# A graph network on one core: the rows of two relational tables as fp32r pairs instead of bf16 triples

## The chip, the cores and the metric

The kernel runs on one core of a Trainium2 chip. The metric is the device time of one execution in microseconds; the time before is the median of three runs.

## The reference, cut to what matters

Four graph layers follow one another on 3125 nodes of 128 features and 100,000 edges (sorted by destination). The change touches only the last of them, a relational network of two layers with eight kinds of edge:

```python
def rgcn_layer(x, src, dst, etype, W, W_root, b, num_rels):
    h = jnp.einsum('ni,rio->rno', x, W)
    msg = h[etype, src]
    seg = dst * num_rels + etype
    sums = jax.ops.segment_sum(msg, seg, num_segments=N * num_rels)
    cnt = jax.ops.segment_sum(jnp.ones(...), seg, num_segments=N * num_rels)
    mean = sums / jnp.maximum(cnt, 1.0)[:, None]
    return mean.reshape(N, num_rels, do).sum(axis=1) + x @ W_root + b
...
h = relu(rgcn_layer(x, src, dst, etype, W1, root1, b1, 8))   # 128 -> 256
y = rgcn_layer(h, src, dst, etype, W2, root2, b2, 8)         # 256 -> 128
x = _layernorm(x + y)
```

So for each node and each kind of edge the features of the source nodes are averaged, and the eight averages, each through its own weights, are added.

## The kernel before, in words

The 3125 nodes are 25 blocks of 128 (`NB`, `P`); a feature matrix lies in SBUF as 25 tiles of 128 nodes by 128 features. From 0 to about 430 us the kernel builds matrices of edge counts (bf16 `adj`, `adj_t`; uint8 `rel`, one for each relation) in HBM. Until about 850 us it runs the first three graph layers as products with `adj`. From there on it runs the two relational layers, and everything that is changed lies there.

**Two ways to sum over edges.** Destination blocks 0 to 14 (`ND = 15`, in chunks `DENSE` of 4, 4, 4 and 3 blocks) are done densely, blocks 15 to 24 by gathering.

*Dense*: `relation` (L873) takes one relation and one chunk. In each of five steps g it loads five source blocks of the uint8 counts (`load8`, SP's queue, L757, six buffers), casts them to fp32r (`cast8`, L767, on ScalarE or VectorE by a list, three buffers), and issues ten matmuls (L885): for each of the five source blocks two, with the hi and the lo fp32r part of the features as the stationary operand and 512 or 384 columns of counts moving. `split2` (L786) makes such a pair: hi is x rounded to fp32r on ScalarE (L789), lo the rest on VectorE (L790). A pair for all 25 blocks is a tile `hilo`, of which two buffers (tag `big`) exist; `hT` has the same tag. In layer 1 the features are x3 itself; in layer 2 each relation r has its own matrix, x3's successor hT times W2[r], which layer 1 has written to HBM.

*Gathered*: `gathered` (L893) is a generator. For each of the ten blocks it walks over 34 tiles of 128 edges (15 for the last block). For four tiles at a time VectorE builds a one-hot (L909) that says to which of 24 x 8 = 192 pairs of node and relation an edge belongs. GpSimd fetches the 128 source rows of a tile from a table in HBM (L919, an indirect DMA, 12 buffers `gx`). TensorE then adds gx times one-hot to an accumulator of 1024 columns in two PSUM banks (L927); where the 192 columns cross the border of the banks (column 512), the matmul is cut in two.

**The two tables.** `xt_d` holds x3, `ht_d` hT times W2 for eight relations. A row is kept as three bf16 parts that add up to the fp32 value, 768 bytes, so a gathered tile takes three bf16 matmuls. `store3` (L792) makes them: a = bf16(x) on ScalarE (L798), e = x - a on VectorE (L799), b = bf16(e) on ScalarE (L800), c = e - b on VectorE (L801), and one store on SP (L802). It is called for seven chunks of x3 (`stored`, L846) and, in `linear1` (L950), for 50 half-rows of four relations straight out of PSUM, after four matmul instructions each (L975; an fp32 product is two instructions in the trace).

**Reading the table densely.** In layer 2 `fetch` (L1018) brings one relation's 25 blocks back: five loads (`back`, two buffers, L1024), two additions on VectorE that rebuild fp32 (L1027, L1028), and `split2` into the pair.

**What sets the order.** `fill` (L866) advances the gathering generator at a rate, so that after each dense step of ten matmuls about two gathered tiles follow. `fetch(r + 1)` is called after the first chunk of relation r. The framework then orders each engine's queue at compile time by priority and its own estimates; in the trace `back` and `m8` loads alternate on SP's queue.

Of the kernel before, what the change touches and what calls it, by code (L numbers as in the profile page):

```python
# [21 lines left out]
P = 128  # L22
# [51 lines left out]
def listed(ctx: ExitStack, tc: tile.TileContext, p: dict, out: bass.AP, bad):  # L74
# [43 lines left out]

    inv_n = dram.tile([SB * 2 * P, R], F32, name="inv_n")

    xt_d = dram.tile([NP, 3 * D], BF, name="xt_d")
    ht_d = dram.tile([R * NP, 3 * D], BF, name="ht_d")

    xa = const.tile([P, NB, D], F32, name="xa")
    iota2 = const.tile([P, R * NB, 2], BF, name="iota2")
# [628 lines left out]
    with until_end:  # L754
# [34 lines left out]
            nc.scalar.copy(hi, x)  # L789
            nc.vector.tensor_sub(lo, x, hi.bitcast(F32))  # L790

        def store3(rows, x):  # L792

            n = x.shape[1]
            t = rp.tile([P, 4, 3, D], BF, name="t3", bufs=4)
            a, b, c = [t[:, :n, i, :] for i in range(3)]
            e = rp.tile([P, 4, D], F32, name="e3", bufs=3)[:, :n, :]
            nc.scalar.copy(a, x)  # L798
            nc.vector.tensor_sub(e, x, a)  # L799
            nc.scalar.copy(b, e)  # L800
            nc.vector.tensor_sub(c, e, b)  # L801
            nc.sync.dma_start(rows, t[:, :n].rearrange("p b i c -> p b (i c)"))  # L802


        def batchnorm(bst, i):
# [38 lines left out]
        hT = rp.tile([P, 2, NP], F32, name="hT", tag="big", bufs=2)  # L844

        def stored(m0, nb):  # L846
            store3(xt_d[m0 * P : (m0 + nb) * P].rearrange("(b p) c -> p b c", p=P), x3[:, m0 : m0 + nb, :])

        for c, (m0, nb) in enumerate(CH):
            t = bank(("acc", "x", "x", "x", "x", "mi", "mi")[c])  # L850
# [42 lines left out]
        def gathered(table, rows, put):  # L893
# [3 lines left out]
            for g in range(NG):  # L897
                b = ND + g
                wn = min(P, HL - b * P)
                iv = rp.tile([P, P * R], F32, name="invn", bufs=1)  # L900
                nc.scalar.dma_start(iv[:, : wn * R],
                                    bcast(inv_n.rearrange("n r -> (n r)")[b * P * R :], wn * R))
                acc = [bank("x") for _ in range(2)]
                seen = set()
                for t in range(GT[g]):
                    if t % 4 == 0:
                        nt = min(4, GM - t)
                        oh = rp.tile([P, 2, GW * R, 2], BF, name="oh", bufs=3)
                        ins = nc.vector.tensor_tensor(  # L909
                            oh[:, : nt // 2],  # L910
                            iota2[:, None, : GW * R, :].to_broadcast([P, nt // 2, GW * R, 2]),
                            gkey[:, g, t : t + nt].rearrange("p (j i) -> p j i", i=2)[:, :, None, :]
                            .to_broadcast([P, nt // 2, GW * R, 2]),
                            op=OP.is_equal,
                        )
                        if g == 0 and t < 12:
                            behind(ins, first_cast)
                    gx = rp.tile([P, 3, D], BF, name="gx", bufs=12)
                    nc.gpsimd.indirect_dma_start(  # L919
                        out=gx.rearrange("p i c -> p (i c)"), out_offset=None, in_=table[:],  # L920
                        in_offset=bass.IndirectOffsetOnAxis(ap=rows[:, g, t : t + 1], axis=0),
                    )
                    c0 = first(t) * R
                    ends = [c0] + ([512] if c0 < 512 < c0 + GW * R else []) + [c0 + GW * R]
                    for i in range(3):
                        for a, z in zip(ends, ends[1:]):
                            nc.tensor.matmul(  # L927
                                acc[a // 512][:, a % 512 : a % 512 + z - a], gx[:, i, :],
                                oh[:, t % 4 // 2, a - c0 : z - c0, t % 2],
                                start=(a // 512 not in seen), stop=(t == GT[g] - 1 and i == 2),  # L930
                                skip_group_check=True,
                            )
                            seen.add(a // 512)
                    yield
                parts = [(n, min(64, wn - n), acc[n // 64][:, : min(64, wn - n) * R],
                          iv[:, n * R : min(wn, n + 64) * R]) for n in range(0, wn, 64)]
                yield from put(b, wn, parts) or ()
                yield

        with tc.tile_pool(name="f_z", bufs=1, reuse_waits="tile") as zp:  # L940
# [9 lines left out]
            def linear1(z, m0, nb):  # L950
# [20 lines left out]
                for b in range(m0, m0 + nb):  # L971
                    for r in range(0, R, 4):
                        o = psum.tile([P, 512], F32, name="mi", tag="mi", bufs=2)
                        for a in range(2):
                            nc.tensor.matmul(o, hT[:, a, cols(b, 1)],  # L975
                                             wr[:, a, r : r + 4, :].rearrange("p r c -> p (r c)"),
                                             start=(a == 0), stop=(a == 1))
                        store3(ht_d.rearrange("(r n) c -> n r c", r=R)[b * P : (b + 1) * P, r : r + 4],
                               blocks(o))
                        yield  # L980

# [35 lines left out]
        with tc.tile_pool(name="f_hr", bufs=1, reuse_waits="tile") as hp:  # L1017
            def fetch(r):  # L1018

                pieces = pair()  # L1020
                for m0 in range(0, NB, 5):
                    t = hp.tile([P, 5, 3, D], BF, name="back", bufs=2)
                    r0 = r * NP + m0 * P
                    nc.sync.dma_start(t.rearrange("p b i c -> p b (i c)"),  # L1024
                                      ht_d[r0 : r0 + 5 * P].rearrange("(b p) c -> p b c", p=P))
                    f = hp.tile([P, 5, D], F32, name="f", bufs=2)
                    nc.vector.tensor_add(f, t[:, :, 0], t[:, :, 1])  # L1027
                    nc.vector.tensor_add(f, f, t[:, :, 2])  # L1028
                    split2(pieces, m0, 5, f)
                return pieces  # L1030

            oT = hp.tile([P, NP], F32, name="oT")
# [670 lines left out]
```

## Time and profile before

| | us |
|---|---|
| median of three runs | 2034.96 (2032.4 to 2036.95) |
| profiled execution, own time | 2027.4 |
| its span | 2025.5 |
| mean granted TensorE clock | 0.975 |
| L885 dense matmuls, 3200 | busy 792.3 |
| L927 gathered matmuls, 2208 | busy 227.1 |
| L767 casts, ScalarE 225 and VectorE 95 | busy 486.8 and 158.5 |
| L919 gathers, 321 in each layer | busy 366.1 and 326.2 |
| L909 one-hots, 170 | busy 90.3 |
| L1027 and L1028 rebuilding, 40 each | busy 32.6 and 32.4 |

The page gives busy time by engine and by line. Matmuls are pipelined, and the busy time of one counts its latency; what a matmul costs in a stream is the distance from one start to the next, which the chain of work in order of time shows. "PEld" is the load of the stationary operand, which can overlap a matmul. A line such as "PE acc L885 <- ACT m L767: 7.9, 14, 1.4" says that matmuls of L885 waited for casts of L767, 7.9 us in all, 14 times, at most 1.4 us.

### The profile page before, as it was taken

What the parts mean: (1) busy time and instruction counts of PE and PEld (TensorE: products, weight loads), DVE (VectorE), ACT (ScalarE), POOL (GpSimd) and SP (SyncE); (2) the same over time, 40 slices, a digit from 0 to 9 for tenths busy, and PEclk for the clock granted to TensorE, in tenths of its full rate; (3) what the DMA queues carried; (4) which work ended last, traced back from release to release, by engine and by line L of the source; (5) the groups of instructions that cost most, each with busy time, mean ns of one, the idle gap of its engine ahead of it and who ended that gap; (6) DMA issues with size and microseconds to landing.
All of it is one profiled execution on the core that took longest, in us unless ns stands there. A gap on an engine that the chain in (4) does not pass through costs nothing.

```text
span 2025.5 us, 30183 instructions
## 1 busy us (share of the span) xinstructions
PE 1794.3 (89%) x11523; PEld 1387.0 (68%) x11523; DVE 1205.1 (59%) x2055; ACT 1253.0 (62%) x1118; POOL 859.5 (42%) x717
## 2 busy tenths in 40 slices
PE   2677676669999999889999999999999999999897
PEld 1555555458888888667577567758757777777676
DVE  6999998777768863475455345435346444434424
ACT  3999997757888666663233333233338777777774
POOL 5315624120000000027777267706716666666664
PEclk9999998889999999999999999999999999999998
DMA  4766776667888887477677457737659887888773
GB/s 100 277 271 266 291 287 237 247 189 232 255 259 257 251 268 235 140 225 190 177 212 207 148 171 209 188 101 198 184 151 269 243 228 220 235 240 245 196 204 101
DMA packets 398932, 435.67 MB, mean 215 GB/s; under 512 B 27166, under 2 KB 355838, under 8 KB 398776
## 3 DMA queue, kind: packets, MB, share of 16 engines
q1 hardware_dynamic: 346274, 336.92, 53.0%
q0 software_dynamic: 33632, 67.07, 12.9%
q10 hardware_dynamic: 18870, 29.66, 4.9%
q8 instruction: 92, 1.51, 0.3%
q14 instruction: 64, 0.52, 0.1%
HBM read 319.07 MB, written 114.46 MB: 214 GB/s over the span
## 4 chain that ended last, share of the span: by engine, by line
PE 57%; ACT 4%; issue 3%; DVE 3%; another core or an unknown queue 2%; DMA 1%; ACTq 0%; SPq 0%; DVEq 0%
PE acc L885 30%; PE acc L628 8%; PE x L927 8%; PE mi L962 4%; PE mi L975 4%; ACT m L767 3%; PE mi L966 1%; DMA back<-ht_d 1%; PE mi L650 0%; PE x L836 0%; PE mi L740 0%; DVE hilo L790 0%; ACT mf L611 0%; DVE f L1027 0%
## 5 line engine op out<-in xcount | busy, mean ns | idle before, releaser
L885 PE MATMUL acc<-m,hilo 128*128 128x512 f32 (+1 forms) x3200 | 792.3, 393 | 22.8 <-ACT m L767 10.8
L767 ACT CAST m<-m 128x2560 fp32r<-128x2560 uint8 (+1 forms) x225 | 486.8, 2196 | 372.5 <-PE acc L885 148.7
L885 PEld LDWEIGHTS acc<-m,hilo 128*128 128x128 f32 x3200 | 576.5, 190 | 130.3 <-issue 17.6
L919 POOL DMA_INDIRECT gx<-xt_d,gsrc x321 | 366.1, 1140 | 638.5 <-DVE z L1007 413.7
L919 POOL DMA_INDIRECT gx<-ht_d,gsrc x321 | 326.2, 1016 | 200.1 <-issue 72.0
L628 PE MATMUL acc<-mf,halves 128*128 128x512 f32 (+1 forms) x1750 | 383.9, 377 | 11.5 <-DVE mf L613 11.0
L628 PEld LDWEIGHTS acc<-mf,halves 128*128 128x128 f32 x1750 | 320.4, 190 | 60.4 <-DVE mf L613 11.9
L611 ACT CAST mf<-m 128x2560 fp32r<-128x2560 bf16 (+1 forms) x126 | 263.7, 2100 | 67.3 <-PE acc L628 34.8
L927 PE MATMUL x<-oh,gx 128*128 128x192 bf16 (+5 forms) x2208 | 227.1, 239 | 5.5 <-issue 5.2
L927 PEld LDWEIGHTS <-gx 128*128 128x128 bf16 x2208 | 157.0, 97 | 99.2 <-issue 89.6
L767 DVE CAST m<-m 128x2560 fp32r<-128x2560 uint8 (+1 forms) x95 | 158.5, 1670 | 110.6 <-issue 40.3
L909 DVE TENSOR_TENSOR oh<-iota,gkey 128x768 bf16<-128x768 bf16 (+1 forms) x170 | 90.3, 532 | 208.5 <-PE x L927 143.2
L342 ACT CAST rb<-bld 128x800 uint16<-128x800 f32 x240 | 180.0, 847 | 6.5 <-PE bld L339 6.5
L339 PE MATMUL bld<-rhq,rlo 128*128 128x200 bf16 x960 | 124.2, 253 | 49.4 <-ACT rb L342 36.5
L290 POOL DMA_INDIRECT ew<-pk,ptr x26 | 72.7, 2797 | 193.9 <-DVE ptr L285 189.6
L339 PEld LDWEIGHTS <-rlo 128*128 128x128 bf16 x960 | 86.9, 98 | 85.3 <-issue 80.9
L613 DVE CAST mf<-m 128x2560 fp32r<-128x2560 bf16 (+1 forms) x49 | 97.5, 1989 | 70.1 <-PE acc L628 69.9
L191 DVE TENSOR_TENSOR lo<-iota,kT 128x4096 bf16<-128x4096 bf16 x50 | 114.2, 2283 | 11.1 <-PE bld L356 11.1
L191 DVE TENSOR_TENSOR rhq<-iota,kT 128x6400 bf16<-128x6400 bf16 x30 | 104.4, 3480 | 0.0
L975 PE MATMUL mi<-wr,hT 128*128 128x512 f32 x200 | 93.4, 601 | 2.5 <-issue 1.6
L359 ACT CAST at<-bld 128x800 bf16<-128x800 f32 x100 | 79.4, 835 | 20.7 <-PE bld L356 20.6
L270 POOL DMA_INDIRECT g<-in_dst,irow x26 | 76.6, 2947 | 22.9 <-DVE crow L265 9.8
(238 smaller groups left out, 1624.4 us busy)
## 6 DMA issues: line engine op xcount, KB each, us to landing
m<-rel SPq DMA_DIRECT2D x240, 320.0 KB
rel<-rb SPq DMA_DIRECT2D x120, 400.0 KB
m<-adj SPq DMA_DIRECT2D x60, 640.0 KB
m<-adj_t SPq DMA_DIRECT2D x40, 640.0 KB
m<-adj SPq DMA_DIRECT2D x45, 480.0 KB
adj_t<-at SPq DMA_DIRECT2D x25, 800.0 KB
adj<-av SPq DMA_DIRECT2D x25, 800.0 KB
ht_d<-t SPq DMA_DIRECT2D x50, 384.0 KB
```

The costliest lines, as they stand in the source:

```text
L191: return nc.vector.tensor_tensor(o, (iota2 if of is None else of)[:, None, :width, :].to_broadcast([P, PU // 2, width, 2]), k[:, :, None, ...
L339: nc.tensor.matmul(pt[:, k, : R * NB], lo2[:, j // 2, :, j % 2], hq[:, j // 2, :, j % 2], start=True, stop=True)
L342: nc.scalar.copy(rb[:, :, j0 : j0 + 4], pt[:, :, : R * NB].rearrange("p j q -> p q j"))
L611: nc.scalar.copy(v, src)
L613: nc.vector.tensor_copy(v, src)
L628: nc.tensor.matmul(acc[:, :w], x[:, 5 * g + k, :], mf[:, k, :w], start=(g == 0 and k == 0 and i == 0), stop=(more is None and g == 4 and k ...
L767: casts_by[on_act] = nc.scalar.copy(v, src) if on_act else nc.vector.tensor_copy(v, src)
L885: nc.tensor.matmul(acc[:, :w], x[:, 5 * g + k, :], m[:, k, :w], start=(g == 0 and k == 0 and i == 0), stop=(g == 4 and k == 4 and i == 1),)
L909: ins = nc.vector.tensor_tensor(oh[:, : nt // 2], iota2[:, None, : GW * R, :].to_broadcast([P, nt // 2, GW * R, 2]), gkey[:, g, t : t + nt ...
L919: nc.gpsimd.indirect_dma_start(out=gx.rearrange("p i c -> p (i c)"), out_offset=None, in_=table[:], in_offset=bass.IndirectOffsetOnAxis(ap ...
L927: nc.tensor.matmul(acc[a // 512][:, a % 512 : a % 512 + z - a], gx[:, i, :], oh[:, t % 4 // 2, a - c0 : z - c0, t % 2], start=(a // 512 no ...
L975: nc.tensor.matmul(o, hT[:, a, cols(b, 1)], wr[:, a, r : r + 4, :].rearrange("p r c -> p (r c)"), start=(a == 0), stop=(a == 1))
```

## The change

Both tables hold fp32 words, two parts of 128 to a row (1024 bytes), each an fp32r part. `store2` takes the place of `store3`: hi on ScalarE, lo on VectorE, one store. The table of x3 is stored from the two parts of `xs`, which exist already, with one DMA each. A gathered tile is two fp32r matmuls; the one-hots are built in fp32r, one tile after the other instead of in interleaved pairs; ten buffers `gx` instead of twelve. `fetch` loads the two parts of a relation straight into the pair, with ten DMAs, and has no arithmetic. Bitcasts to fp32 on both sides of the DMAs leave the bytes as they are.

```diff
@@ -118,8 +118,8 @@
 
     inv_n = dram.tile([SB * 2 * P, R], F32, name="inv_n")
 
-    xt_d = dram.tile([NP, 3 * D], BF, name="xt_d")
-    ht_d = dram.tile([R * NP, 3 * D], BF, name="ht_d")
+    xt_d = dram.tile([NP, 2 * D], F32, name="xt_d")
+    ht_d = dram.tile([R * NP, 2 * D], F32, name="ht_d")
 
     xa = const.tile([P, NB, D], F32, name="xa")
     iota2 = const.tile([P, R * NB, 2], BF, name="iota2")
@@ -789,17 +789,14 @@
             nc.scalar.copy(hi, x)
             nc.vector.tensor_sub(lo, x, hi.bitcast(F32))
 
-        def store3(rows, x):
+        def store2(rows, x):
 
             n = x.shape[1]
-            t = rp.tile([P, 4, 3, D], BF, name="t3", bufs=4)
-            a, b, c = [t[:, :n, i, :] for i in range(3)]
-            e = rp.tile([P, 4, D], F32, name="e3", bufs=3)[:, :n, :]
-            nc.scalar.copy(a, x)
-            nc.vector.tensor_sub(e, x, a)
-            nc.scalar.copy(b, e)
-            nc.vector.tensor_sub(c, e, b)
-            nc.sync.dma_start(rows, t[:, :n].rearrange("p b i c -> p b (i c)"))
+            t = rp.tile([P, 4, 2, D], F32R, name="t2", bufs=3)
+            hi, lo = [t[:, :n, i, :] for i in range(2)]
+            nc.scalar.copy(hi, x)
+            nc.vector.tensor_sub(lo, x, hi.bitcast(F32))
+            nc.sync.dma_start(rows, t[:, :n].rearrange("p b i c -> p b (i c)").bitcast(F32))
 
 
         def batchnorm(bst, i):
@@ -844,7 +841,9 @@
         hT = rp.tile([P, 2, NP], F32, name="hT", tag="big", bufs=2)
 
         def stored(m0, nb):
-            store3(xt_d[m0 * P : (m0 + nb) * P].rearrange("(b p) c -> p b c", p=P), x3[:, m0 : m0 + nb, :])
+            rows = xt_d[m0 * P : (m0 + nb) * P].rearrange("(b p) (i c) -> i p b c", p=P, i=2)
+            for i, x in enumerate(xs):
+                nc.sync.dma_start(rows[i], x[:, m0 : m0 + nb, :].bitcast(F32))
 
         for c, (m0, nb) in enumerate(CH):
             t = bank(("acc", "x", "x", "x", "x", "mi", "mi")[c])
@@ -905,29 +904,28 @@
                 for t in range(GT[g]):
                     if t % 4 == 0:
                         nt = min(4, GM - t)
-                        oh = rp.tile([P, 2, GW * R, 2], BF, name="oh", bufs=3)
+                        oh = rp.tile([P, 4, GW * R], F32R, name="oh", bufs=3)
                         ins = nc.vector.tensor_tensor(
-                            oh[:, : nt // 2],
-                            iota2[:, None, : GW * R, :].to_broadcast([P, nt // 2, GW * R, 2]),
-                            gkey[:, g, t : t + nt].rearrange("p (j i) -> p j i", i=2)[:, :, None, :]
-                            .to_broadcast([P, nt // 2, GW * R, 2]),
+                            oh[:, :nt],
+                            iota2[:, None, : GW * R, 0].to_broadcast([P, nt, GW * R]),
+                            gkey[:, g, t : t + nt, None].to_broadcast([P, nt, GW * R]),
                             op=OP.is_equal,
                         )
                         if g == 0 and t < 12:
                             behind(ins, first_cast)
-                    gx = rp.tile([P, 3, D], BF, name="gx", bufs=12)
+                    gx = rp.tile([P, 2, D], F32R, name="gx", bufs=10)
                     nc.gpsimd.indirect_dma_start(
-                        out=gx.rearrange("p i c -> p (i c)"), out_offset=None, in_=table[:],
+                        out=gx.rearrange("p i c -> p (i c)").bitcast(F32), out_offset=None, in_=table[:],
                         in_offset=bass.IndirectOffsetOnAxis(ap=rows[:, g, t : t + 1], axis=0),
                     )
                     c0 = first(t) * R
                     ends = [c0] + ([512] if c0 < 512 < c0 + GW * R else []) + [c0 + GW * R]
-                    for i in range(3):
+                    for i in range(2):
                         for a, z in zip(ends, ends[1:]):
                             nc.tensor.matmul(
                                 acc[a // 512][:, a % 512 : a % 512 + z - a], gx[:, i, :],
-                                oh[:, t % 4 // 2, a - c0 : z - c0, t % 2],
-                                start=(a // 512 not in seen), stop=(t == GT[g] - 1 and i == 2),
+                                oh[:, t % 4, a - c0 : z - c0],
+                                start=(a // 512 not in seen), stop=(t == GT[g] - 1 and i == 1),
                                 skip_group_check=True,
                             )
                             seen.add(a // 512)
@@ -975,7 +973,7 @@
                             nc.tensor.matmul(o, hT[:, a, cols(b, 1)],
                                              wr[:, a, r : r + 4, :].rearrange("p r c -> p (r c)"),
                                              start=(a == 0), stop=(a == 1))
-                        store3(ht_d.rearrange("(r n) c -> n r c", r=R)[b * P : (b + 1) * P, r : r + 4],
+                        store2(ht_d.rearrange("(r n) c -> n r c", r=R)[b * P : (b + 1) * P, r : r + 4],
                                blocks(o))
                         yield
 
@@ -1018,15 +1016,10 @@
             def fetch(r):
 
                 pieces = pair()
+                rows = ht_d[r * NP : (r + 1) * NP].rearrange("(b p) (i c) -> i p b c", p=P, i=2)
                 for m0 in range(0, NB, 5):
-                    t = hp.tile([P, 5, 3, D], BF, name="back", bufs=2)
-                    r0 = r * NP + m0 * P
-                    nc.sync.dma_start(t.rearrange("p b i c -> p b (i c)"),
-                                      ht_d[r0 : r0 + 5 * P].rearrange("(b p) c -> p b c", p=P))
-                    f = hp.tile([P, 5, D], F32, name="f", bufs=2)
-                    nc.vector.tensor_add(f, t[:, :, 0], t[:, :, 1])
-                    nc.vector.tensor_add(f, f, t[:, :, 2])
-                    split2(pieces, m0, 5, f)
+                    for i, x in enumerate(pieces):
+                        nc.sync.dma_start(x[:, m0 : m0 + 5, :].bitcast(F32), rows[i][:, m0 : m0 + 5])
                 return pieces
 
             oT = hp.tile([P, NP], F32, name="oT")
```

## The prediction

> **What bounds the kernel now.** I read the page first: busy shares, then the chain that ended last.
>
> ```profile
> PE 1794.3 (89%) x11523; PEld 1387.0 (68%) x11523; DVE 1205.1 (59%) x2055; ACT 1253.0 (62%) x1118; POOL 859.5 (42%) x717
> PE 57%; ACT 4%; issue 3%; DVE 3%; another core or an unknown queue 2%; DMA 1%; ACTq 0%; SPq 0%; DVEq 0%
> ```
>
> TensorE holds the chain. The change begins at about 854 us (x3) and ends with the program, so I then read the chain in order of time inside the two relational layers (861 to 1521 and 1521 to 2025 us).
>
> ```profile
> 1100.66 2.36 PE acc L885 x10
> 1103.02 0.53 PE x L927 x6
> 1103.55 2.36 PE acc L885 x10
> ...
> 1179.15 0.56 PE x L927 x12
> ...
> 1503.27 2.00 PE mi L962 x16
> ...
> 1505.49 1.79 PE mi L962 x16
> ...
> 1507.50 1.78 PE mi L975 x4
> ```
>
> These give the spacing of matmuls, which is what PE pays. A dense fp32r product of 512 columns: 236 ns. Six gathered bf16 matmuls (two tiles) of 192 columns: 88 ns each. Twelve of a tile pair cut at column 512 of the accumulator: 47 ns each. An fp32 pass (the trace has two for each fp32 product) of 64 columns: 112 ns. One of 512 columns: 429 to 445 ns. Tiles and dense steps alternate without a gap, so a nanosecond of gathered matmul is a nanosecond of layer 1.
>
> Last, what PE waits for in layer 2, and the DMA load there (columns: window, PE, PEld, DVE, ACT, POOL busy, clock, DMA share, GB/s).
>
> ```profile
> PE mi L1042 <- DVE oT L1061: 8.3, 2, 5.8
> PE acc L885 <- ACT m L767: 7.9, 14, 1.4
> PE acc L885 <- issue: 6.4, 15, 1.0
> PE x L927 <- issue: 4.7, 9, 0.9
> ...
> PE acc L885 <- DVE hilo L790: 1.1, 1, 1.1
> ```
> ```profile
> 1550.00:1600.00 50.00, 48.01 (x293) 38.64 (x293) 24.28 (x38) 41.13 (x24) 35.60 (x34) 1.00 0.88 254
> 1750.00:1800.00 50.00, 47.92 (x288) 37.96 (x287) 24.46 (x43) 39.11 (x23) 33.81 (x34) 1.00 0.89 253
> ```
>
> PE idles about 33 us in all of layer 2, and the DMA engines are nearly full. So PE is the bound, with DMA close behind in layer 2 alone.
>
> **What the Trainium skill says.** "TensorE: Matmul & The Clock Gate", LDWEIGHTS: a load takes its columns over 1.2 GHz, so 107 ns for 128; the section on weight-path modes adds that the fast load is for types other than FP32. The trace agrees: fp32 loads last 190 ns, bf16 ones 97, and the 112 ns of a 64-column fp32 pass is far above its 53 ns of columns (as 429 ns for 512 scales), so the load sets it. "VectorE: DVE Perf Modes", what auto-detection checks: two results a cycle for two-source operations only where every tensor is 16-bit. The trace agrees: 768 bf16 elements take 553 ns (L909), 640 with an fp32 output 824 (L1027). "DMA: Bandwidth & Descriptors", issuing engines are not separate queues: all queues share the same 16 engines. The trace agrees, in that one DMA share covers SP's, ACT's and POOL's.
>
> **The change, part by part.** Durations are of the profiled execution: 2027.4 us, a span of 2025.5 and 1.9 around it. The median is 2034.96, 7.6 more, which I add at the end.
>
> *Gathered matmuls (L927).* Two parts instead of three. There are 2208 now = 642 tiles x 3 + 94 tiles cut in two x 3. Now: 548 whole tiles x 3 x 88 = 145 us, 94 cut ones x 6 x 47 = 26, together 171. After: 548 x 2 + 94 x 4 = 1472. No fp32r matmul in the trace is narrower than 384 columns (178 ns, 10 in 1.78 us on the chain), so I bound it. From below: the columns at the 384-column rate, 89 ns, less than the load, so 112 ns: 1472 x 0.112 = 165 us, 6 less than now. From above: as an fp32 product, two passes of 0.84 ns a column, 322 ns for 192: 548 x 2 x 322 = 353, the cut ones 65 with the load as floor, together 418 us, **247 more**. I take 112: fp32r ran in one pass at 384 and 512 with nearly the same ns a column (0.46), so nothing shown makes a narrower one run twice. **-6 us**.
>
> *One-hots (L909).* Output in fp32, so one result a cycle at 1.08 ns an element (from 512 in 686 to 640 in 824): 768 in 962 ns, +409 on 152, about +200 on 18: +66 us of DVE in both layers, and nothing at the other end (unchanged 553). DVE is busy 20 to 29 of 50 us there, and three buffers of four tiles run ahead of PE: 0 on the path. If that cover went, each tile would pay 0.1 us, 66 us in all; since a pair of tiles comes every 2.9 us on PE, I count nothing.
>
> *x3 stage.* store3's two ACT and two DVE steps for seven chunks go (t, e, t: 0.5 to 0.69 us each): 8 us of ACT and 9 of DVE. From 861 to 876 us DVE is solidly busy and PE's L885 has gaps of 2.2, 0.9, 0.3, 0.2 and 1.4 us, 5 in all; then it runs 119 products without one. The cast ends that last gap, so not all goes: **-4 us**. SP issues 14 stores in place of 7, 0.36 us each: 2.5 us ahead of m8 loads whose next casts have six buffers.
>
> *store2 (50 blocks of linear1).* L800 (0.62) and L801 (0.69) go. PSUM is still freed after one ACT and one DVE read, L798 0.58 and L799 0.69. Now ACT's L800 waits for L799 ahead of the next L798: 0.58 + 0.69 + 0.62 = 1.9 us a block against 1.72 on PE (4 x 429). Afterwards 1.3. The waits PE shows for it are 3.7 us (DVE e 2.1, issue 1.6); the last store before layer 2 also leaves 1.3 sooner. **-4 us**. Stores of 512 KB for 384: 25600 packets at 46 ns for 36 in the trace, 16 us of the 16 engines in layer 1, where their share is 0.44 to 0.79: hidden.
>
> *Fetch.* L1027, L1028, L790 (40 x 0.82 each, 97 us of DVE) and L789 (28 us of ACT) go. What PE waits for in layer 2 is only partly theirs: hilo 1.1, casts behind hilo copies some of 7.9 and 6.4. I credit 5 us. Against it: 80 DMAs of 320 KB for 40 of 480. Each now writes the hilo pair itself, so **SP waits** for the last L885 of the relation two before, where ACT and DVE did; behind it on SP's queue stand the m8 loads (L757), for them ACT's casts, for those PE. Packets in the trace: 768 B take 36 ns, 512 B 27. 25600 x 36 becomes 51200 x 27: over 16 engines 58 to 86 us, +29. I take -5 from the freed engines and +5 from this: 0.
>
> *Gathers (L919).* 1024 B a row for 768. POOL's issue is by row (0.95 us, a pitch of 1.25), so unchanged. One engine's share is now packets of 1536 and 4608 B, 65 + 221 = 286 ns; a third more, 381: +31 us of DMA in each layer. Ten gx buffers for twelve still reach seven steps of 2 tiles less two: about 14 us ahead, where a gather needs a few. 0 on the path.
>
> Sum: -6 - 4 - 4 + 0 = -14, so 2013 for the profiled execution and **2020** for the median.
>
> **Rivals.**
> 1. *Narrow fp32r matmuls run at the fp32 rate* (slower). +247 us on PE; about 20 of it fills idle time of layer 2, and 8 of savings stay: 2027.4 + 247 - 20 - 8 = 2246, median about **2250**. For it: no fp32r product under 384 columns is shown. Against it: the constant ns a column above. It decides as soon as a 192-column product costs over about 130 ns (1472 x 0.018 = 26 us above my price, more than the other savings). A halfway price (165 ns) would give some 2095.
> 2. *DMA becomes the bound of layer 2.* Now 0.777 of 514 us = 399 us there; + 29 + 31 = 459, 0.89. In the stretch with fetches, at 0.80 to 0.89 now, it is 0.96. One fetch is 6400 packets x 27 / 16 = 10.8 us of all engines, 15 beside the gathers, as one burst ahead of the m8 loads, whose six buffers hold 6 x 2.9 = 17 us less what SP waits for PE. If that wait is a step or two, PE stalls up to 6 us in each of seven relations, +42: 2020 + 42 - 5 = about **2057**. For it: the shares. Against it: the order on SP is interleaved already (back and m8 loads alternate in the queue's timeline), and a chunk's first pieces are needed first.
> 3. *Nothing much moves*: the gathered matmuls cost 124 ns, savings off the path: **2035**.
>
> **How the numbers follow.** Forecast 0.48, rival 1 (all prices well over 130 ns) 0.27, rival 2 0.19, rival 3 0.06. The forecast's own range is 2004 to 2031. For 8 in 10 the range must take in rival 2 and half of rival 1: 2004 to 2250, which leaves out 0.14 above and some 0.04 below. 0.2% is 4 us, about what a measurement tells from no change. Faster 0.45 (0.03 of the forecast falls within 0.2%), same 0.09, slower 0.46.
>
> **What would show it.** Right: six gathered matmuls (0.53 us) become four in 0.45 between dense steps of 2.36; L909 about 960 ns; no gaps at 861 to 876; layer 1 shorter by 10 us or more; layer 2 within 10 us of its 504 with a DMA share near 0.9. Wrong: four gathered in 0.6 us or more (rival 1), or "PE acc L885 <- ACT m L767" of tens of us in layer 2, with casts waiting for m<-rel behind hilo<-ht_d (rival 2).

## The result and the profile after

| | before | after |
|---|---|---|
| median of 20 runs each, same chip | 2032.0 us (2024.1 to 2037.69) | 2037.74 us (2027.13 to 2043.84) |
| ratio after to before | | 1.0029 (95% 1.0016 to 1.0042) |
| span of the profiled execution | 2025.5 | 2037.6 |
| mean granted TensorE clock | 0.975 | 0.964 |

The kernel is slightly slower, by 0.3%. I had forecast 12 to 15 us less. Lines of the changed kernel carry other numbers: dense products L884, gathered ones L925, casts L767, the ten loads of a fetch L1022, linear1's products L960 and L973.

The page first: busy shares and the chain.

```profile
PE 1786.8 (88%) x10787; PEld 1439.2 (71%) x10787; DVE 1143.3 (56%) x1871; ACT 1195.0 (59%) x1014; POOL 853.8 (42%) x717
PE 54%; issue 3%; ACT 3%; DMA 2%; another core or an unknown queue 2%; DVE 2%; SPq 1%; ACTq 0%; POOLq 0%; DVEq 0%
```

PE's part of the chain falls from 57 to 54%, though the span grows: PE has less to do and waits more. The chain in order of time, in the dense part of layer 1:

```profile
1095.63 2.35 PE acc L884 x10
1097.98 0.42 PE x L925 x4
1098.40 2.34 PE acc L884 x10
...
1103.69 0.42 PE x L925 x4
```

Four gathered matmuls in 0.42 us, 105 ns each, where six took 0.53. The same view at the end of layer 1, where the kernel before had sixteen 64-column passes in 1.79 us:

```profile
1492.64 3.45 DMA gx<-xt_d,gsrc
...
1496.86 4.44 DMA gx<-xt_d,gsrc
...
1503.97 3.31 PE mi L960 x16
```

PE waits for gathers, and afterwards a pass costs 207 ns instead of 112. Last, layer 2: PE's waits (us in all, times, longest), and three stretches (same columns as before, the last three are clock, DMA share, GB/s).

```profile
PE acc L884 <- ACT m L767: 18.4, 12, 6.1
PE acc L884 <- issue: 8.8, 7, 3.9
PE x L925 <- issue: 6.7, 8, 3.5
```
```profile
1550.00:1600.00 50.00, 46.54 (x242) 40.47 (x241) 15.01 (x21) 34.24 (x17) 32.42 (x34) 0.93 0.88 242
1650.00:1700.00 50.00, 43.62 (x219) 37.41 (x218) 11.47 (x15) 32.54 (x16) 31.35 (x31) 0.90 0.91 256
1750.00:1800.00 50.00, 46.29 (x239) 39.66 (x240) 15.58 (x31) 34.51 (x18) 33.99 (x34) 0.97 1.00 290
```

The waits for casts are not many, 12 instead of 14, but long: up to 6.1 us for 1.4. And the clock, which was 1.00, is 0.90 to 0.97.

**Where the time went.** I cut both traces at the starts of matmuls: the first and last dense product of layer 1, the product for oT (hT times the root weights, with which layer 2 begins; its own 10.3 to 10.6 us stand in no row), and the dense products of layer 2 by relation. "Half clock" is the time for which the trace's clock record shows TensorE at half speed; for layer 2 it takes in a last piece of 9 to 13 us, which reaches 2 us past the program's end. The pair on the right (runs e13 and e14 below) was taken on another chip, side by side.

| us | before | after | e13, before | e14, after |
|---|---|---|---|---|
| dense part of layer 1 | 590.3 | 580.3 | 587.8 | 578.6 |
| end of layer 1 (last dense product to product for oT) | 59.4 | 74.5 | 62.1 | 72.8 |
| relation 0, after that product | 55.6 | 51.7 | 55.2 | 51.7 |
| relations 1 to 7 | 434.9 | 443.1 | 425.4 | 442.8 |
| from there to the end | 13.6 | 16.4 | 13.2 | 16.6 |
| half clock: end of layer 1 | 0 | 20.5 | 3.4 | 20.5 |
| half clock: layer 2 | 26.5 | 51.2 | 12.1 | 50.2 |

So the predicted 10 us of the dense part came, and were given back at the end of layer 1 and in layer 2.

### The profile page after: what moved, and what is told of

The parts are those of the page before. It is cut to its first block, busy times and chain, and to the rows that moved or that the text cites. A ratio compares the mean times of both kernels' runs of the same rounds, so it can differ in the third digit from the quotient of the medians.

```text
span 2037.6 us, 28569 instructions
## 1 busy us (share of the span) xinstructions
PE 1786.8 (88%) x10787; PEld 1439.2 (71%) x10787; DVE 1143.3 (56%) x1871; ACT 1195.0 (59%) x1014; POOL 853.8 (42%) x717
## 4 chain that ended last, share of the span: by engine, by line
PE 54%; issue 3%; ACT 3%; DMA 2%; another core or an unknown queue 2%; DVE 2%; SPq 1%; ACTq 0%; POOLq 0%; DVEq 0%
PE acc L884 29%; PE acc L628 7%; PE x L925 7%; PE mi L960 4%; PE mi L973 4%; ACT m L767 2%; SPq L1022 1%; DMA m<-rel 1%; PE mi L964 1%; PE mi L1029 1%; DMA hilo<-ht_d 0%; DMA gx<-xt_d,gsrc 0%; PE mi L650 0%; DMA inv<-inv_d 0%
## 5 line engine op out<-in xcount | busy, mean ns | idle before, releaser
L884 PE MATMUL acc<-m,hilo 128*128 128x512 f32 (+1 forms) x3200 | 778.9, 390 | 34.9 <-ACT m L767 19.7
L767 ACT CAST m<-m 128x2560 fp32r<-128x2560 uint8 (+1 forms) x225 | 486.2, 2196 | 414.9 <-PE acc L884 130.0
L884 PEld LDWEIGHTS acc<-m,hilo 128*128 128x128 f32 x3200 | 581.5, 192 | 136.7 <-ACT m L767 22.2
L917 POOL DMA_INDIRECT gx<-xt_d,gsrc x321 | 370.4, 1154 | 646.9 <-PE acc L884 408.5
L908 DVE TENSOR_TENSOR oh<-iota,gkey 128x768 fp32r<-128x768 bf16 (+1 forms) x170 | 154.9, 913 | 275.1 <-PE x L925 171.6
L925 PEld LDWEIGHTS x<-oh,gx 128*128 128x128 f32 x1472 | 216.8, 193 | 52.2 <-issue 23.8
L925 PE MATMUL x<-oh,gx 128*128 128x192 f32 (+5 forms) x1472 | 228.2, 280 | 13.3 <-issue 6.7
L767 DVE CAST m<-m 128x2560 fp32r<-128x2560 uint8 (+1 forms) x95 | 159.1, 1676 | 88.8 <-issue 28.9
L191 DVE TENSOR_TENSOR lo<-iota,kT 128x4096 bf16<-128x4096 bf16 x50 | 114.1, 2282 | 13.0 <-PE bld L356 11.6
L973 PE MATMUL mi<-wr,hT 128*128 128x512 f32 x200 | 94.7, 615 | 5.9 <-issue 5.9
L798 DVE TENSOR_TENSOR t<-mi,t 128x512 fp32r<-128x512 f32 x50 | 34.5, 691 | 110.4 <-ACT t L797 87.9
```

Of the source, the lines that this page charges most:

```text
L191: return nc.vector.tensor_tensor(o, (iota2 if of is None else of)[:, None, :width, :].to_broadcast([P, PU // 2, width, 2]), k[:, :, None, ...
L767: casts_by[on_act] = nc.scalar.copy(v, src) if on_act else nc.vector.tensor_copy(v, src)
L884: nc.tensor.matmul(acc[:, :w], x[:, 5 * g + k, :], m[:, k, :w], start=(g == 0 and k == 0 and i == 0), stop=(g == 4 and k == 4 and i == 1),)
L908: ins = nc.vector.tensor_tensor(oh[:, :nt], iota2[:, None, : GW * R, 0].to_broadcast([P, nt, GW * R]), gkey[:, g, t : t + nt, None].to_bro ...
L917: nc.gpsimd.indirect_dma_start(out=gx.rearrange("p i c -> p (i c)").bitcast(F32), out_offset=None, in_=table[:], in_offset=bass.IndirectOf ...
L925: nc.tensor.matmul(acc[a // 512][:, a % 512 : a % 512 + z - a], gx[:, i, :], oh[:, t % 4, a - c0 : z - c0], start=(a // 512 not in seen), ...
```

## The experiments

**Theory A.** (i) At the end of layer 1, 13 gathered tiles of the last block stand behind the last but one linear1 in PE's order; ten buffers hold ten of them, and PE waits for the rest. (ii) In layer 2 a fetch is now ten loads in one go; SP is held up by them, the counts behind them come late, then the casts, then PE. Later I added (A2) that a long wait of PE is followed by half clock. **Rivals**: the DMA engines' bytes bound layer 2; the order set at compile time and the clock make the end of layer 1 longer, not the buffers; the inv loads on ScalarE's queue, behind which casts stand, are what is late in layer 2.

The chain in order of time of the changed kernel shows one such fetch, and SP's queue its issues:

```profile
1652.99 2.00 SPq L1022
...
1655.04 2.49 SPq L1022
...
1657.58 8.24 DMA hilo<-ht_d
...
1665.90 0.33 ACTq L779
...
1669.95 2.33 ACT m L767
...
1672.33 4.64 PE acc L884 x10
```
```profile
1636.48 9.35 SPq L757 DMA_DIRECT2D m<-rel  x3
1645.88 16.51 SPq L1022 DMA_DIRECT2D hilo<-ht_d  x10
1662.50 17.74 SPq L757 DMA_DIRECT2D m<-rel  x10
```

A load of counts takes SP 0.36 us to issue, a load of the fetch 1.4 at the median and up to 4.0; ten hold SP for 16.5 us. The first load of counts after them leaves at 1662.5, and the cast that needs it starts at 1669.95, 7.4 later. 24 us without counts against six buffers of 2.8 us each leaves PE some 7 us short; it waits 6.1, and its next ten products take 4.64 us instead of 2.35. In the kernel before the same queue alternates:

```profile
1588.77 1.17 SPq L1024 DMA_DIRECT2D back<-ht_d  x2
1590.59 3.85 SPq L757 DMA_DIRECT2D m<-rel  x2
1596.07 0.36 SPq L1024 DMA_DIRECT2D back<-ht_d  x1
1596.53 0.49 SPq L757 DMA_DIRECT2D m<-rel  x1
```

Times below are ratios to the kernel before on the same chip, with 95% intervals. The runs fell on five chips, on which the kernel before took 2021.5 (e1 to e4), 2030.8 (e5 to e8), 1968.5 (e9 to e12), 2019.4 (e13 to e16) and 2031.2 us (e17, e18). The unaltered changed kernel was run beside e5 to e8 and e13 to e16 alone; elsewhere its 1.0029 to 1.0057 are from other chips. Stage times are from one profiled execution each, and that can lie off the median: by 5 us in e2 and e3, and by 11 in e4, whose profile is the slowest of its 13 runs.

**e1: twelve buffers.**
```diff
-gx = rp.tile([P, 2, D], F32R, name="gx", bufs=10)
+gx = rp.tile([P, 2, D], F32R, name="gx", bufs=12)
```
To make room, root2 is loaded later and `m` has a smaller pad.


> The changed kernel with twelve gx buffers instead of ten; to make room, root2 is loaded in the second layer's pool and the pad of m is 4 instead of 8. Theory A (the end of layer 1 pays for the two missing buffers: 13 tiles of the last block are left after the last but one linear1, ten are there, three are fetched while PE waits): the stretch from the last dense product of layer 1 to the product for oT falls from 85 to about 77 us, and the median by 6 to 8, to about 2031. Theory B (the end of layer 1 is longer because of the slower TensorE clock and the order set at compile time): at most 2 us, about 2036. Theory C (everything that was lost lies in layer 2): within 1 us of 2037.


Measured: 1.0036 (1.0022 to 1.0051). The stretch of 85 us, which counts the oT product itself, became 81. PE takes 8.4 us for the last gathered tiles instead of 10.5, of which waits for gathers are 3.7 instead of 4.8 (the expectation of e6 calls the whole 10.5 and 8.4 a wait). The time shows no gain. Half of what theory A said in the trace, nothing in the ratio.

**e2: ten buffers in the kernel before.**
```diff
-gx = rp.tile([P, 3, D], BF, name="gx", bufs=12)
+gx = rp.tile([P, 3, D], BF, name="gx", bufs=10)
```


> The kernel before with ten gx buffers instead of twelve, nothing else. Theory A: its last block has twelve tiles left at that place, ten are there, two must be fetched while PE waits, so the 70 us of the end of layer 1 become 75 to 77 and the median 2032 becomes about 2038. Theories B and C: within 1.5 us of 2032.


Measured: 1.0020 (1.0011 to 1.0030), about 4 us; the 70 us became 79. The timeline of PE:

```profile
1503.41 0.43 PE L927 MATMUL x<-oh,gx 128*128 128x128 bf16 x6 [1.88 <-DMA gx<-xt_d,gsrc]
1503.68 0.30 PE L956 MATMUL mi<-ident,xa 128*128 128x128 f32 x1
1504.93 3.50 PE L962 MATMUL mi<-zg,w 128*128 128x64 f32 x16 [0.94 <-DVE zg L991]
```

The missing two buffers cost 1.9 us of waiting, and then the 64-column passes take 3.50 us instead of 2.00: the clock is half for 10 us. This, alone in the kernel before, is the loss at the end of layer 1 in small. The 79 is from a profile 5 us above the median, so the ratio is the safer size.

**e3: the fetch spread.** One load after each dense step of chunks 1 and 2.
```diff
-for m0 in range(0, NB, 5):
-    for i, x in enumerate(pieces):
-        nc.sync.dma_start(...)
+def parts():
+    for m0 in range(0, NB, 5):
+        for i, x in enumerate(pieces):
+            nc.sync.dma_start(...)
+            yield
...
 fill(work, rate)
+next(each, None)
```


> The changed kernel with the ten loads of a fetch issued one after each dense step of chunks 1 and 2 instead of all after chunk 0; same bytes, same packets, same number of DMAs. Theory A (the burst holds SP's queue and the semaphores of earlier DMAs, so the uint8 counts and the inv loads come late): the long chunks 1 of relations 2, 5, 6 and 7 (20 to 25 us) go back to 14 to 17, relations 1 to 7 take 435 instead of 443 us, median about 2030. Rival (the DMA engines are the bound of layer 2 by their bytes): no change, 2036 to 2039. If SP's order makes the next relation's first piece late, slower: 2045.


Measured: 1.0003 (0.9989 to 1.0018), relations 1 to 7 in 436.9 us. Near what theory A said: with the same bytes some 5 us less than the changed kernel's 1.0029, which is from another chip. But not every long chunk 1 went: that of relation 6 took 23.8 us, that of relation 7 19.0.

**e4: hi and lo side by side.** Five loads with 1024-byte packets.
```diff
-t = rp.tile([P, 2, NB, D], F32R, name="hilo", tag="big", bufs=2)
+t = rp.tile([P, NB, 2, D], F32R, name="hilo", tag="big", bufs=2)
```


> The changed kernel with hi and lo of a block side by side in SBUF, so that a fetch is five DMAs with 1024-byte packets instead of ten with 512, still all at once; the store of x3 is one DMA for a chunk instead of two. Packet time of the fetches falls from 2 x 27 to 46 ns a row, 15 per cent of 86 us, 13 us of all engines in layer 2. Theory A (burst: number of issues and of semaphores held): about half of the loss of layer 2 comes back, 4 us, median 2033. Rival (bytes and packets of the DMA engines bound layer 2): as much as the share falls, 0.025 of 440, up to 11 us, median 2027. Neither: 2036 to 2039.


Measured: 1.0018 (1.0003 to 1.0033), relations 1 to 7 in 440.1. The bytes rival wanted 0.998 and is not seen; A wanted 1.0005, and the third reading, that nothing changes, fits as well.

**e5: the changed kernel again.**


> The changed kernel once more, unaltered, as a second profile and as the base for the runs beside it. Expected by all theories: 1.003 of the kernel before. What it tells is how far one profile repeats: if the clock drops of TensorE are part of the cause (theory A2: each wait of PE of more than about 2 us is followed by 3.4 us or more at half clock), it shows again some 15 to 20 us of half clock at the end of layer 1 and 40 to 55 us in layer 2, where the first profile had 20.5 and 51.2 and the kernel before 0 and 26.5. If those were chance, they differ widely.


Measured: 1.0057 (1.0033 to 1.0081). The stages repeat within 2 us (582.4, 75.7, 443.0), and the half clock with them: 23.9 us at the end of layer 1, 51.1 in layer 2. The drops are no chance.

**e6: fifteen buffers.**
```diff
-gx = rp.tile([P, 2, D], F32R, name="gx", bufs=10)
+gx = rp.tile([P, 2, D], F32R, name="gx", bufs=15)
-oh = rp.tile([P, 4, GW * R], F32R, name="oh", bufs=3)
+oh = rp.tile([P, 4, GW * R], F32R, name="oh", bufs=2)
```


> The changed kernel with fifteen gx buffers (all tiles of the last block can be there at once); room is made by two one-hot buffers instead of three, by root2 in the second layer's pool and by a pad of 4 in m. With twelve buffers the wait for gathers at the end of layer 1 only fell from 10.5 to 8.4 us. Theory A2: now it falls to about 3 us as in the kernel before, the clock does not drop there, and the stretch from the last dense product to the product for oT goes from 74.5 to 60 to 64 us; median about 10 us under the changed kernel, 0.998 of before. Rival (buffers are not what is missing, the gathers themselves are late because DMA or GpSimd is): the wait stays over 6 us and the median within 2 us of the changed kernel.


Measured: 1.0026 (1.0012 to 1.0040), beside 1.0057 for the changed kernel. The timeline of PE (its lines L923 and L958 are L925 and L960):

```profile
1485.68 2.00 PE L923 MATMUL x<-oh,gx 128*128 128x192 f32 x13
1488.51 2.19 PE L923 MATMUL x<-oh,gx 128*128 128x192 f32 x18 [0.84 <-DVE oh L906]
...
1491.79 2.00 PE L958 MATMUL mi<-zg,w 128*128 128x64 f32 x16 [0.23 <-DVE zg L987]
```

No wait for a gather is left, and the passes are back at full clock. The stretch is 66.3 us instead of 75.7 (e5); A2 had said 60 to 64.

The stretch as a whole is a rough measure: from the last dense product to the next transposes it takes 27 to 38 us in the traces, whatever the buffers, since PE's waits inside linear1 differ. Cut at the first of the last block's remaining tiles, the rest up to the product for oT is plain: 12.2 us in both traces of the kernel before, 18.5 in e2, 23.9 to 25.2 in all ten traces with ten buffers and both parts, always with 17.1 us of half clock, and 17.2 or 17.3 in e6, e11, e15 and e18, without any, although 13 more products of layer 2 (3 us) stand there. Two traces stand apart: e1 with twelve buffers (26.3, of which 3.8 are such products) and e12, which waits 4.6 us for root2 there (23.4). The buffers are the cause of this part.

About half of the expected gain shows in the ratio. The trace says where the rest went: relation 0 has one wait of 4.3 us and 6.8 us of half clock that e5 lacks, and takes 55.1 us after the oT product instead of 51.5. That leaves 5.8 of 9.4 us, 0.003, which is what the ratio moved.

**e7: both alterations of the fetch**, one 640 KB load at every second dense step.


> The changed kernel with both of the earlier alterations of the fetch: five loads with 1024-byte packets instead of ten, and one of them issued at every second dense step of chunks 1 and 2. Theory A2 (the burst holds SP and the semaphores; PE waits a few us and then runs at half clock): relations 1 to 7 take 430 to 434 us where the changed kernel took 443, half clock in layer 2 falls from 51 to 25 to 35 us, median 0.998 to 0.9995 of before. Rival (DMA bytes): only the 13 us of engine time of the packets count, 1.001 to 1.002 as with the 1024-byte packets alone.


Measured: 1.0003 (0.9990 to 1.0016). Relations 1 to 7 in 433.0, half clock 34.6 us: as A2 said for the stages. The ratio is 0.001 above its span, and spreading alone had given the same.

**e8: ten buffers for counts in layer 2.**
```diff
-m8 = rp.tile([P, 4, 5, P], U8, name="m8", bufs=6)
+m8 = mp[0].tile([P, 4, 5, P], U8, name="m8", bufs=mp[1])
```


> The changed kernel with ten buffers for the uint8 counts in layer 2 instead of six (28 us ahead of PE instead of 17); the fetch still comes as one burst. Theory A2, in the form that the counts come late because SP spends 17 to 24 us on the ten fetches and the loads behind them: the deeper queue rides it out, long chunks 1 vanish, relations 1 to 7 take about 433 us, ratio 0.999. Rival form (what is late is the inv load on ScalarE's queue, which waits for a fetch's semaphore with the casts behind it): no help, 1.003. The DMA bound: no help either.


Measured: 1.0018 (1.0006 to 1.0029), relations 1 to 7 in 438.9, under half of the distance to 433. PE's longest wait for a cast fell from 4.0 to 1.9 us; the half clock stayed at 49.7.

**e9: hi part alone multiplied** (the lo part's gathered matmuls are left out).
```diff
-for i in range(2):
+for i in range(1):
     for a, z in zip(ends, ends[1:]):
```


> The changed kernel with only the hi part of a gathered tile multiplied: it leaves out the lo part's matmuls of both layers (736 of 1472, some 77 us of PE at 105 ns), and gathers and loads the same bytes. It asks what a microsecond of gathered matmul is worth in each layer. Where PE is the bound, all of it comes back: about 35 us in the dense part of layer 1 (582 to 547). In layer 2, theory A2 (PE has long waits there and would have more, with more half clock): less than half, relations 1 to 7 from 443 to not under 428. Rival (layer 2 is bound by PE as I predicted, only disturbed): 443 to about 410.


Measured: 1.0018 (1.0007 to 1.0029). 77 us less work for PE, and still slower than the kernel before. The dense part of layer 1 took 557.3 us; the other three kernels of this chip took 571 to 572, so 15 us came back, not 35, since PE then waits 15.1 us for gathers. Relations 1 to 7 took 409.5, which is the rival's figure and under my 428; but both were reckoned from slower chips and say nothing here.

**e10: hi part alone fetched** (the lo part's loads are left out, and hi is multiplied twice).
```diff
-for i, x in enumerate(pieces):
+for i, x in enumerate(pieces[:1]):
     nc.sync.dma_start(...)
...
-return pieces
+return [pieces[0], pieces[0]]
```


> The changed kernel with only the hi part of a relation fetched, five loads instead of ten, and the dense products of layer 2 made with hi in both places: it leaves the lo part out of layer 2's dense product; PE, ScalarE and VectorE have the same work. 1.6 MB and 43 us of all engines less. Theory A2 (burst) and the DMA bound both expect less: A2 that relations 1 to 7 come to 432 or so, as with the spread loads of 1024-byte packets, which moved all bytes; the DMA bound that they fall well under that, to 415 or less, since the share goes from 0.96 to 0.86.


Measured: 0.9989 (0.9982 to 0.9996). Relations 1 to 7: 388.2 us, against 409.5 in e9, though PE multiplies twice as many gathered parts. PE's waits in layer 2, e9 and then e10:

```profile
PE acc L884 <- ACT m L767: 34.5, 6, 7.7
PE x L925 <- DMA gx<-ht_d,gsrc: 13.4, 16, 2.0
```
```profile
PE mi L1035 <- DVE oT L1054: 4.1, 4, 1.7
PE mi L1035 <- DVE oT L1071: 3.3, 4, 1.0
PE x L925 <- DMA gx<-ht_d,gsrc: 3.0, 2, 2.2
```

Six waits of some 6 us for casts with ten loads, and none with five: chunk 1 takes 17 to 24 us in relations 1 to 6 of e9, 14 to 15 in e10. By itself this doesn't part burst from bytes; e11 and e12 do.

**e11 and e12: the repairs together** (e4's layout, paced as in e7, buffers as in e6), and with e8's buffers.


> The changed kernel with hi and lo side by side and the five loads of a fetch at every second dense step of chunks 1 and 2, and with fifteen gx buffers (two one-hot buffers, root2 later, pad 4). The two repairs lie in different stages and should add: end of layer 1 about 66 us, relations 1 to 7 about 433, so 6.6 and 3.2 us under the changed kernel, 0.997 to 0.999 of the kernel before. If they don't add, 1.000 to 1.002.

> The same with ten buffers for the uint8 counts in layer 2. Ten buffers alone took 4 us off layer 2 of the changed kernel. If they and the paced loads cure the same wait, nothing is added: within 2 us of the kernel without them. If each leaves a rest, 2 to 4 us less, 0.996.


Measured: 0.9962 (0.9949 to 0.9975) and 0.9990 (0.9980 to 1.0000). Relations 1 to 7 took 394.6 and 388.8 us, half clock in layer 2 15.1 and 11.6. e12 moves all bytes, at a DMA share of 0.97 to 0.99, as fast as e10, which leaves out half of each fetch: **on this chip the bytes are not the bound**. Why e12's median is above e11's, with equal spans in the profiles, stays open.

**e13 to e15: side by side on one chip**, the kernel before, the changed kernel, e11's kernel.


> The kernel before, unaltered, for a trace on the same chip as the runs beside it. Expected: ratio 1.000; end of layer 1 about 59 us from the last dense product to the product for oT, no chunk 1 of layer 2 over 18 us, at most some 30 us of half clock in layer 2.

> The changed kernel, unaltered, on the same chip. If the two losses are the cause everywhere: dense part of layer 1 8 to 10 us shorter than in the kernel before beside it, end of layer 1 14 to 16 us longer, relations 1 to 7 8 us or more longer with several chunks 1 over 20 us, ratio 1.002 to 1.006. If they belong to the slower chips only: layer 2 at least as fast as before, ratio under 1.

> The changed kernel with the loads of a fetch paced and paired and with fifteen gx buffers, again. 0.996 to 0.999 of the kernel before: dense part of layer 1 as in the changed kernel, end of layer 1 62 to 66 us, relations 1 to 7 at most as long as in the kernel before.


Measured: 0.9998 (0.9985 to 1.0011), 1.0047 (1.0029 to 1.0065), 0.9986 (0.9971 to 1.0000). PE's waits in layer 2, e13 and then e14:

```profile
PE acc L885 <- ACT m L767: 11.0, 12, 3.1
PE acc L885 <- issue: 7.4, 16, 0.9
```
```profile
PE acc L884 <- ACT m L767: 24.8, 16, 5.3
PE acc L884 <- issue: 4.9, 5, 3.4
```

Five of the seven relations of e14 after the first have a chunk 1 of 19 to 25 us; in e13 only one is over 18 (20). By the table above, 9 us are gained in the dense part and 3.5 in relation 0; 11, 17 and 3 us are lost at the end of layer 1, in relations 1 to 7 and at the end. In e15 the end of layer 1 is 65.1, as expected, and relations 1 to 7 are 428.6: 14 less than in e14, but 3 more than in e13, where I had said at most as long. So the repairs take back what the change had lost, and leave little of what it should have won.

**e16 and e17: inv loads on GpSimd's queue**, in both layers and in layer 2 alone; **e18**: e11's kernel with the latter.
```diff
-nc.scalar.dma_start(t[:, : nb * P], bcast(v, nb * P))
+nc.gpsimd.dma_start(t[:, : nb * P], bcast(v, nb * P))
```


> The changed kernel with the inv loads issued by GpSimd instead of ScalarE, so that no cast stands behind a load that waits for a fetch's semaphore; the fetch is still one burst. If the inv loads are a part of the loss: long chunks 1 get shorter by some 3 us each, relations 1 to 7 take 438 us where the changed kernel takes 443 (on a chip where that is so), ratio about 0.002 under the changed kernel. If only the late counts matter: no change. If GpSimd's gathers suffer from 64 more loads at about a microsecond each, 2 to 5 us slower.

> The changed kernel with the inv loads of layer 2 alone on GpSimd's queue. If casts behind an inv load are a part of the loss: relations 1 to 7 take 436 to 438 us where the changed kernel took 443, layer 1 is as in the changed kernel (end of layer 1 73 to 75 us), ratio 1.001 to 1.003. If the gain of the run before came from elsewhere: 443 and 1.004.

> The kernel with the fetch paced and paired, fifteen gx buffers, and the inv loads of layer 2 on GpSimd's queue. If pacing and the moved loads cure the same wait: as without the move, 0.9985 (0.9962 was seen too). If each leaves a rest: relations 1 to 7 under 425 us on a chip where the kernel before takes 425 to 435, ratio 0.994 to 0.997.


Measured: 1.0113 (1.0083 to 1.0143), 1.0035 (1.0016 to 1.0054), 1.0010 (0.9996 to 1.0023). In e16 relations 1 to 7 took 436.1, which looked like a gain; in e17, where layer 1 is left alone, they took 446.8, and in e18 437.0. No gain repeats, so the inv loads are not shown to be part of the loss. The chain above says why they need not be: ScalarE's inv load (L779) goes out at 1665.9, and the cast still starts at 1669.95. In e16 the dense part of layer 1 took 583.1 us and its end 78.6, for 578.6 and 72.8 in e14; PE waits 3.9 us for gathers in that dense part, and e14 shows no such wait. That the gathers queue behind the loads on GpSimd is my reading of it. In e18 the end of layer 1 took 74.6 us in spite of fifteen buffers: 7.7 of them are one wait for ScalarE's hT in linear1, ahead of the last tiles.

## Why the prediction was wrong

*Gathered matmuls.* Right, and better than priced: 105 ns, not 112; 1472 x 0.105 = 155 us instead of 171, so -16 for -6. Rival 1 is out. But e9 shows the limit of "a nanosecond of gathered matmul is a nanosecond of layer 1": after some 15 us more, the gathers are late.

*One-hots.* 955 ns for the 962 priced, and PE's list of waits has none for them in the changed kernel: right.

*x3 stage.* The first chunk took 17.2 us for 20.2: -3 for -4. *store2.* Its -4 I can't show: from the last dense product to the next transposes PE took 34.4 us instead of 30.7, with two waits of 1.5 and 3.0 us in linear1's products (in e14 32.1, in e13 33.5). With the gathered part of layer 1, the dense part came out at -9 to -10.

*Gathers: "Ten gx buffers for twelve still reach seven steps of 2 tiles less two: about 14 us ahead, where a gather needs a few. 0 on the path."* **This step failed.** It counts a steady stage. At the end of layer 1 there are no dense steps between the tiles; there the buffers are all that is ahead, and 13 tiles stand in a row. e2 and e6 show it from both sides, counted from the first of these tiles to the product for oT: two buffers fewer take the kernel before from 12.2 to 18.5 us, five more take the changed one from 24.7 to 17.3. In e14 this piece is 13 us longer than in e13, more than the whole 11 lost at the end of layer 1. In the changed kernel's first trace only 4.8 us of it are waits for gathers; the rest goes with the half clock, 17.1 us of it in this piece.

*Fetch: "I take -5 from the freed engines and +5 from this: 0."* **This step failed too**, and with it the argument against rival 2, "the order on SP is interleaved already". It was interleaved because a `back` load had to wait for one of two buffers, as SP's waits in layer 2 of the kernel before show (us in all, times, longest):

```profile
SPq L1024 <- DVE f L1028: 26.0, 17, 2.9
```

The change takes the buffers away and so the pacing. I counted a wait of SP for PE; what held SP was issuing, 1.4 us a load. A spread load is hardly cheaper (1.2 us at the median in e3); what pacing changes is how many of them stand ahead of the counts. Rival 2 had the right place and chain, but its name was wrong (on the chip of e10 to e12 the DMA engines are not the bound; on the slower ones no run takes bytes away) and its +42 was too much: 8 and 17 us in relations 1 to 7.

*Half clock* is in no step of mine: I put it at nothing without a reason. The Trainium skill, "TensorE: Matmul & The Clock Gate", the part on the HAM clock gate, says that after an idle window of about 3.4 us the array runs at half clock until it has been busy for one such window. The traces agree on the size and on long waits: the record's half-clock stretches come in pieces of 3.4 us, and in all twenty traces, from the first dense product on, every one of 66 waits of PE of 3 us or more has one that overlaps it or begins within 3.5 us after it. They differ in two things. 151 of 283 waits of 1 to 3 us, shorter than such a window, have one as well. And it can last longer than one window: at the end of layer 1 the changed kernel stays at half clock until 1514.1, 12.8 us after PE's last wait there. 38 us more of it in layer 2 (e14 against e13) are at most 19 us of PE's time, beside a sum of listed waits that grew from 31 to 45. Waits and drops overlap, so I don't divide the 17 us between them. What the runs show is that the drops go where the long waits go (e10, e11, e12).

*Layer 2's own gain* is real, but hidden by this. Relation 0 is 3.5 to 3.9 us shorter, of which 0.7 are three products done ahead of the oT product. In relations 1 to 7 PE's waits are 26 us in e13 and 40 in e14, its half clock 3 and 38; with the waits and half of the half clock taken off, 398 us are left of 425 and 384 of 443. That is an estimate, but it says that PE's own work there fell by some 14 us while the waits and the clock cost twice that. So it was luck, and no sign of a right account, that layer 2 as a whole (511 us for 504) stayed within the 10 us that the prediction had named.

What stays open: why one chip runs every version 50 to 60 us faster. Between e11 and e15, the same kernel, 42 of 54 us lie in layer 2; in relations 1 to 7 PE waits 11 us instead of 33 and has 3 us of half clock instead of 21, which covers most of the 34 us there, but why it waits less isn't shown.

## What to carry to other kernels

When a staging buffer goes, ask what it paced: the two `back` buffers kept SP's queue alternating, and without them a whole matrix stood ahead of the loads that PE needs next. Count buffers at the ends of stages, where nothing else covers them, and not only in the steady state. And prefer many short waits of TensorE to a few long ones: here every wait of 3 us or more had half clock beside it, and about half of those of 1 to 3 us.

## What the runs showed that I had not expected

A narrow fp32r matmul of 192 columns runs in 105 ns between dense ones. A 320 KB load in 512-byte rows takes SP 0.36 us to issue on a free queue, and 1.4 us at the median (up to 4.0) in a burst of ten, 1.2 when the ten are spread (e3). A wait of 1.9 us with 0.9 more behind it (e2) was enough for 10 us of half clock in a stretch of small products.
